# Four graph layers in one plan, mask terms of 256 columns, and biases off TensorE

## The chip, the cores and the metric

The kernel runs on one core of a Trainium2 chip. The core has a matrix engine (TensorE, PE in the profile), a vector engine (VectorE, DVE), a scalar engine for activations (ScalarE, ACT), a general engine (GpSimd, POOL) and a queue that issues DMA transfers (SyncE, SP). The metric is device time of one launch in microseconds; the median over repeated runs is given. Times of single instructions come from one profiled execution.

## The reference

The input is 32 graphs of 512 nodes with 128 features each, one adjacency matrix of 512 x 512 that all graphs share, and the weights of four layers. All numbers are float32. Each layer takes `h = relu(layernorm(x))` and adds its result to `x`:

```
# layer 0: attention over paired scores; softmax over the column's entries
h  = x @ others_weight;  e = leaky_0.1(u1[:, idx1] + u2[:, idx2])
out = softmax(where(adj > 0, e, NEG), axis=1) @ h + x @ self_weight
# layer 1: attention, then a graph network with a two-layer MLP
h = x @ Wp + bp
attn = softmax(where(A <= 0, min, leaky_0.2(s_src[:, None] + s_dst[None, :])))
h_gat = relu(layernorm((attn * A) @ h, g, b))
z = relu(layernorm(((1 + eps) * h_gat + A @ h_gat) @ W1 + b1, g, b))
out = relu(z @ W2 + b2 + h_gat)
# layer 2: attention, elu
out = elu(softmax(where(adj > 0, leaky_0.2(f1[:, None] + f2[None, :]), NEG)) @ (x @ W) + bias)
# layer 3: two projections mixed by one 512 x 512 softmax A that all graphs share
out = diag(A) * (x @ W0) + offdiag(A) @ (x @ W1) + bias
```

In layer 0 the paired indices make the scores of the second 256 nodes (rows) independent of the row: for these rows the attention weight of a column is one number per column where the adjacency has an edge, and nothing elsewhere.

## The kernel before

All 32 graphs stay in SBUF in `xs`, as four blocks of 128 nodes by 128 features per graph. A constant part prepares transposed adjacency (`adjT`), masks, weights with two score columns appended (`w0_ext`, `w1_ext`, `w2_ext`, 130 columns), and layer 3's shared attention matrix (`offT`, `adiag`).

Work is not written in loops that run in order. Each layer of each graph is a *chain* of operations: `op(engine, length, emit, reads, writes)` puts one on a list with an assumed length, and `Plan.run` then goes through all of them, takes at each step the operation that could begin first by its own running estimate (among those within 0.05 us the one with the earliest *turn*, a due time), and emits its instructions. That order is fixed with dependencies, so each engine executes its instructions in the order in which the plan emitted them. Two things limit the choice: a window of chains (`WINDOW = 7`; no chain more than seven past the oldest unfinished one may start), and rooms of buffers. A room is a pool with a count: `banks` are the eight PSUM banks, `scored` 5, `scores` 8, `turned` 4, `by_pool` 5, `by_act` 6 and `by_dve` 5 tiles in SBUF. The two preparing chains, `prepare` and `prepare_last`, run *beside* the others with due times of their own (`PREPARED`, `FILLED`) and leave two PSUM banks free.

The chains are listed as 32 graphs of layer 0 (due every 6.6 us), then 32 of layer 1 (every 13.3), then layers 2 and 3 together, layer 3 four graphs behind layer 2 (7.0 and 6.0).

Every layer begins with `preln`: mean and variance on DVE (`variances`), a power of -0.5 on GpSimd (`inv_dev`), normalisation on GpSimd (`xn`), four transposes on PE, and a relu on ACT into `hT`. Then:

- `layer0` projects `hT` with 130 columns (`project_scored`, four blocks), sends the score columns to another arrangement by four small DMAs (`u`), computes exponentials (`y`) for the first 256 nodes' weights, and scales the projected rows into two copies: `hs` by the sums for the first half and `hs2` for the second. `emit_po` (lines 776 and 784) then sums in one PSUM bank: per block of rows one matmul of `hT` with the self weight, and four with `y` (first two blocks) or with `mask2T`, a 0/1 mask (last two). DVE adds all of it to `xs` at line 790.
- `layer1` uses `project_scored` and `attend` (scores, exponentials, transposes, product with `adjT`, `po` at line 640), a layer norm from PSUM, the product with `adjTe` (`pg`, line 834), and two projections `pz` and `px` (line 535). Its biases `bp` and `b1` enter on PE: each is split into three bf16 terms in rows 0 to 2 of a tile (`b3_p`, `b3_1`), and a matmul of these with a tile that has ones in three rows (`ones3`) opens the sum: line 552 with 260 columns, twice, and line 530 with 512.
- `layer2` is `attend` without weights, and the elu. `layer3` multiplies the transposed input with the diagonal (`own`), projects (`p1`), and sums `own` and `offT` products (lines 897 and 901); DVE adds the residual (`yo`), and SP stores it.

Of the kernel before, what the change touches and what calls it, by code (L numbers as in the profile page):

```python
# [27 lines left out]
BF16 = mybir.dt.bfloat16  # L29
AF = mybir.ActivationFunctionType  # L30
# [3 lines left out]
P = 128  # L34
# [4 lines left out]
WINDOW = 7  # L39
# [14 lines left out]
PREPARED, FILLED = (40.0, 1.0), (400.0, 4.0)  # L54

RAMP, LAG = 4.0, 4
# [41 lines left out]
class Plan:  # L98
# [44 lines left out]
    def run(self):  # L143
# [15 lines left out]
        for _ in range(len(self.ops)):  # L159
# [3 lines left out]
            for engine, ops in ready.items():  # L163
                could = []
                for op in ops:
# [11 lines left out]
                    for room, n in rooms.items():  # L177
                        if len(room.free) < n + (room.reserve if beside else 0):
                            begin = None
                            break  # L180
# [49 lines left out]
def kernel(  # L230
# [110 lines left out]
    mask2T = const("mask2T", (P, C, N2))  # L341
# [12 lines left out]

    b3_p = const("b3_p", (P, P2), BF16)
    b3_1 = const("b3_1", (P, P), BF16)
    ones3 = const("ones3", (P, P), BF16)
# [8 lines left out]
    v_bias, v_w1, v_w2, v_wz, v_b3, v_adjTe, v_rows, v_mlp = (Value() for _ in range(8))  # L366
# [158 lines left out]
    def project(hT, w, reads, b3=None, name="p"):  # L525
        pt = value(banks, name)

        def emit():
            if b3 is not None:
                nc.tensor.matmul(  # L530
                    pt.t, lhsT=ones3, rhs=b3.rearrange("p (o f) -> p o f", o=1).to_broadcast([P, C, P]),
                    start=True, stop=False,
                )
            for c in range(C):
                nc.tensor.matmul(  # L535
                    pt.t[:, c, :], lhsT=column(hT, c), rhs=w,
                    start=(b3 is None), stop=(b3 is None or c == C - 1),
                )

        op(PE, 0.9 + (0.22 if b3 is not None else 0.0), emit, [hT, *reads], [pt])  # L540
        return pt

    def project_scored(hT, w_ext, reads, b3=None):

        h = parts(scored, "h", 2)
        for k in range(2):
            pt = value(banks, "proj")

            def emit(k=k, pt=pt):
                p = pt.t.rearrange("p (c t) f -> p c (t f)", c=2)[:, :, 0:P2]  # L550
                if b3 is not None:
                    nc.tensor.matmul(
                        p, lhsT=ones3, rhs=b3.rearrange("p (o f) -> p o f", o=1).to_broadcast([P, 2, P2]),
                        start=True, stop=False,
                    )
                for c in range(2):
                    nc.tensor.matmul(  # L557
                        p[:, c, :], lhsT=column(hT, 2 * k + c), rhs=w_ext,
                        start=(b3 is None), stop=(b3 is None or c == 1),
                    )  # L560

            op(PE, 0.46 + (0.11 if b3 is not None else 0.0), emit, [hT, *reads], [pt])
# [686 lines left out]
```

## Time and profile before

| | us |
|---|---|
| median of 3 runs | 1117.56 (1116.08 to 1118.26) |
| the profiled execution | 1114.53 |
| its span from first to last instruction | 1112.8 |
| PE busy in layer 0's stretch, 112 to 224 us | 112.00 of 112 |
| PE busy in layer 1's stretch, 280 to 600 us | 316.3 of 320 |
| PE busy in layers 2 and 3, 760 to 1000 us | 239.99 of 240 |

The profile is one execution. A row of the cost table gives a line of the kernel, the engine, the output and inputs by name, their shapes, the count, the busy time (overlaps counted once) and the mean length of one instruction. Matmuls are pipelined and overlap, so a row's mean is longer than the distance between two of them. PEld is the loading of the stationary operand, which runs beside PE. Each f32 matmul appears as two pairs of PEld and PE; a transpose appears as one. In the table of slices each digit is a tenth of a fortieth of the span. The last words of a row say what the engine waited for before it.

### The profile page before, as it was taken

The page shows a single profiled execution, that of the slowest core. Times are in us where ns is not written, and L with a number is a line of the kernel's source. Part 1 is how long each engine was busy: PE and PEld are TensorE (multiplying, and loading weights), DVE is VectorE, ACT ScalarE, POOL GpSimd, SP SyncE. Part 2 cuts the span into 40 slices and gives each one's busy share as a digit, 9 for nine tenths or more (in the row PEclk, how much of TensorE's full clock was granted, in tenths as well). Part 3 has the DMA queues.
Part 4 walks back from the last instruction along what each step waited for, and adds up shares of the span by engine and source line. Part 5 has one row for each costly group of instructions (what it writes and reads, how often), then busy time and mean ns, then how long its engine had stood idle before and what let it go on. Part 6 is the DMA issues. An engine that isn't in the chain of part 4 may idle for free.

```text
span 1112.8 us, 25144 instructions
## 1 busy us (share of the span) xinstructions
PE 1085.5 (98%) x8680; PEld 989.0 (89%) x8683; DVE 922.5 (83%) x3822; ACT 672.1 (60%) x1588; POOL 673.2 (60%) x1040
## 2 busy tenths in 40 slices
PE   5999999999999999999999999899999999999998
PEld 4899999998787877887788887899999999999997
DVE  8989899978889898998989897977777777777772
ACT  3456455567365565574656765866667766766661
POOL 8355454554546555646456555687776777777773
PEclk8899999999999999999999999999999999999999
DMA  7202210000000000000000000000100000000001
GB/s 189 58 11 50 43 36 2 2 2 2 1 1 1 1 1 1 1 1 1 1 1 2 1 1 1 1 20 20 30 21 20 21 20 20 20 21 29 21 21 39
DMA packets 56911, 20.50 MB, mean 18 GB/s; under 512 B 21584, under 2 KB 56272, under 8 KB 56784
## 3 DMA queue, kind: packets, MB, share of 16 engines
q1 hardware_dynamic: 56784, 18.90, 6.9%
q8 instruction: 69, 1.13, 0.4%
q14 instruction: 58, 0.48, 0.1%
HBM read 10.43 MB, written 8.39 MB: 17 GB/s over the span
## 4 chain that ended last, share of the span: by engine, by line
PE 75%; DVE 16%; ACT 3%; POOL 2%; issue 1%; SPq 1%; DMA 1%; POOLq 0%; ACTq 0%; DVEq 0%
PE po L640 16%; PE pt L386 13%; PE po L784 10%; PE po L901 10%; PE proj L557 6%; PE pg L834 5%; DVE y L587 4%; PE prow L386 3%; PE po L776 2%; ACT y L620 2%; DVE st L475 2%; PE po L897 2%; PE p L535 2%; DVE pT L629 2%; PE pz L535 1%
## 5 line engine op out<-in xcount | busy, mean ns | idle before, releaser
L640 PE MATMUL po<-h,pT 128*128 128x128 f32 x2048 | 244.2, 275 | 1.7 <-DVE pT L379 1.0
L510 POOL TENSOR_SCALAR xn<-xs,nmean,rstd 128x128 f32<-128x128 f32 x512 | 232.0, 469 | 19.7 <-DVE st L475 9.6
L640 PEld LDWEIGHTS po<-h,pT 128*128 128x128 f32 x2048 | 236.3, 192 | 5.8 <-issue 1.9
L620 ACT ACTIVATE y<-y,nmax 128x512 f32<-128x512 f32 x256 | 181.7, 712 | 41.1 <-DVE nmean L501 20.1
L612 ACT ACTIVATE y<-y,h 128x512 f32<-128x512 f32 x256 | 165.4, 712 | 37.4 <-DVE rmax L587 37.1
L489 POOL TENSOR_TENSOR rstd<-ve,mhalf 128x4 f32<-128x4 f32 x160 | 163.9, 1024 | 13.4
L587 DVE CUSTOM_DVE_ANT_0 y<-prow,bias 128x512 f32<-128x512 f32 x256 | 161.9, 683 | 9.5 <-PE prow L386 9.0
L519 ACT ACTIVATE hT<-pt 128x512 f32<-128x512 f32 x128 | 75.5, 591 | 125.0 <-PE pt L386 123.2
L386 PE MATMUL pt<-ident,y 128*128 128x128 f32 x1024 | 135.1, 274 | 2.5 <-ACT y L620 1.8
L901 PE MATMUL po<-h,offT 128*128 128x128 f32 x1024 | 135.4, 275 | 0.5 <-ACT h L377 0.5
L487 POOL TENSOR_SCALAR ve<-mv 128x4 f32<-128x4 f32 x160 | 36.7, 229 | 160.9 <-DVE rsum L756 57.7
L386 PEld LDWEIGHTS pt<-ident,y 128*128 128x128 f32 x1024 | 115.7, 141 | 20.0 <-ACT y L620 11.4
L834 PE MATMUL pg<-adjTe,hg 128*128 128x512 f32 x256 | 128.2, 593 | 0.0
L901 PEld LDWEIGHTS po<-h,offT 128*128 128x128 f32 x1024 | 124.6, 192 | 0.6 <-ACT h L377 0.6
L475 DVE BATCH_NORM_STATS2 st<-xs 128x6 f32<-128x128 f32 x512 | 109.9, 276 | 1.5 <-POOL xs L879 1.4
L557 PE MATMUL proj<-w_ext,hT 128*128 128x130 f32 x768 | 107.8, 279 | 2.3 <-ACT hT L519 2.3
L557 PEld LDWEIGHTS proj<-w_ext,hT 128*128 128x128 f32 x768 | 97.7, 194 | 6.7 <-ACT hT L519 2.9
L377 ACT COPY h<-proj 128x260 f32<-128x260 f32 x192 | 67.6, 371 | 46.3 <-PE proj L557 40.5
L879 POOL TENSOR_TENSOR xs<-xs,em 128x512 f32<-128x512 f32 x32 | 40.9, 1278 | 81.2 <-DVE em L878 81.2
L386 PE MATMUL pt<-ident,xn 128*128 128x128 f32 x512 | 85.2, 279 | 2.7 <-POOL xn L510 1.9
L629 DVE TENSOR_TENSOR pT<-pt,adjT 128x512 f32<-128x512 f32 x128 | 82.1, 680 | 3.4 <-PE pt L386 3.2
L742 ACT ACTIVATE y<-y,nmax 128x256 f32<-128x256 f32 x128 | 63.8, 501 | 31.1 <-DVE rs L760 14.0
(189 smaller groups left out, 2101.2 us busy)
## 6 DMA issues: line engine op xcount, KB each, us to landing
xs<-in_x_dram SPq DMA_DIRECT2D x32, 256.0 KB, 3.6
out_dram<-yo SPq DMA_DIRECT2D x32, 256.0 KB, 2.2
u<-h SPq DMA_DIRECT2D x128, 0.5 KB, 1.8
bias<-in_adj_dram SPq DMA_DIRECT2D x4, 256.0 KB, 3.3
wts<-in_L_gnn_W_dram SPq DMA_DIRECT2D x3, 64.0 KB, 3.8
rows<-in_L_gnn_bias_dram SPq DMA_DIRECT2D x2, 64.0 KB, 3.3
wt_o<-L_gnn_others_weight_dram SPq DMA_DIRECT2D x1, 64.0 KB, 2.3
wts<-n_L_gnn_self_weight_dram SPq DMA_DIRECT2D x1, 64.0 KB, 3.8
```

The source lines that it names most:

```text
L386: nc.tensor.transpose(dst(k), src(k), ident)
L475: nc.vector.bn_stats(st[:, c, :], src(c))
L489: nc.gpsimd.tensor_tensor(rstd.own, ve, mhalf, ALU.pow)
L510: nc.gpsimd.tensor_scalar(xn.t[:, c, :], src[:, c, :], nmean.own[:, c : c + 1], rstd.own[:, c : c + 1], ALU.add, ALU.mult,)
L557: nc.tensor.matmul(p[:, c, :], lhsT=column(hT, 2 * k + c), rhs=w_ext, start=(b3 is None), stop=(b3 is None or c == 1),)
L587: nc.vector.tensor_tensor_reduce(wide(y[ib].t), wide(prow.t), bias[:, ib, :], 1.0, LOWEST, ALU.add, ALU.max, rmax.own[:, ib : ib + 1],)
L612: nc.scalar.activation(yw, yw, AF.Prelu, alpha=0.2, bias=h[0].t[:, ib, P : P + 1])
L620: nc.scalar.activation(yw, yw, AF.Exp, bias=nmax.own[:, ib : ib + 1], accum_out=ssum[0].own[:, ib : ib + 1])
L640: nc.tensor.matmul(po[ib].t[:, ib, :], lhsT=pT.t[:, jb, :], rhs=h[0].t[:, jb, 0:P], start=(jb == 0), stop=(jb == C - 1),)
L784: nc.tensor.matmul(po[ib].t[:, ib, :], lhsT=w, rhs=(hs if ib < H else hs2).t[:, jb, :], start=False, stop=(jb == C - 1),)
L834: nc.tensor.matmul(wide(pg.t), lhsT=hg.t[:, nb, :], rhs=adjTe[:, nb, :], start=(nb == 0), stop=(nb == C - 1))
L901: nc.tensor.matmul(po[ib].t[:, ib, :], lhsT=offT[:, jb, blk(ib)], rhs=h1.t[:, jb, :], start=False, stop=(jb == C - 1),)
```

## The change

Four things change.

1. **Order.** The chains of all four layers are listed together: for each step, layer 0 of graph n, layer 1 of graph n-5, layer 2 of n-10 and layer 3 of n-13. The window is 20 chains, and chains three or more past the oldest unfinished one must leave one tile in each room (`KEPT`). `prepare_last` is due from 150 us on and no longer from 400.
2. **Layer 0's second half.** `hs2` is cut by a bit mask (`cut`, 12 low bits cleared, on DVE) and the rest taken by a subtraction on GpSimd; ACT copies the cut part. Both lie side by side in tiles `hl` of type float32r, and `mask2T` is float32r too: one matmul with 256 moving columns gives the sums of both parts. The first and the second two blocks of rows now have a PSUM bank each (`po_1`, `po_2`). ACT copies the sums of the small parts out (`rest`), DVE adds the two banks' main parts to `xs` in two additions, and GpSimd adds `rest`.
3. **Layer 1's first bias.** The matmuls of line 552 go. GpSimd adds the centred `row_p` to the projected features in place, and DVE adds the constant `score_p` to the source scores (`src`); `attend` is told where its scores come from.
4. **Layer 1's second bias.** The matmul of line 530 goes. DVE adds `row_1` to `pz` on its way out of PSUM (`zn`); the variance is taken from `zn`, and ACT scales it by `rz` in four activations where DVE multiplied. The splitting into bf16 terms in `prepare` goes.

```diff
-WINDOW = 7
+WINDOW = 20
+OLD, KEPT = 3, 1
...
-PREPARED, FILLED = (40.0, 1.0), (400.0, 4.0)
+PREPARED, FILLED = (40.0, 1.0), (150.0, 1.5)
+GAPS, LAGS = (5.7, 12.9, 7.2, 5.8), (0, 5, 10, 13)
...
-                        if len(room.free) < n + (room.reserve if beside else 0):
+                        if len(room.free) < n + (room.reserve if beside else KEPT if order[k] >= oldest + OLD else 0):
...
-    mask2T = const("mask2T", (P, C, N2))
+    mask2T = const("mask2T", (P, C, N2), F32R)
...
-                if b3 is not None:
-                    nc.tensor.matmul(
-                        p, lhsT=ones3, rhs=b3.rearrange("p (o f) -> p o f", o=1).to_broadcast([P, 2, P2]),
-                        start=True, stop=False,
-                    )
...
+        cut = value(by_dve, "cut")
+        op(DVE, 0.35, lambda: nc.vector.tensor_scalar(
+            cut.t.bitcast(I32), hs2.t.bitcast(I32), -4096, None, ALU.bitwise_and), [hs2], [cut])
+        hi, lo = [], []
+        for hf in range(H):
+            pair = parts(turned, "hl", 2)
+            hi.append(pair[0])
+            lo.append(pair[1])
...
+        def hl(hf):
+            return wide(hi[hf].t).bitcast(F32R).rearrange("p (c t f) -> p c t f", c=H, t=2)
...
+        for hf in range(H):
+            own = slice(hf * H, hf * H + H)
+            op(ACT, 0.31, lambda hf=hf, own=own: nc.scalar.copy(hl(hf)[:, :, 0, :], cut.t[:, own, :]), [cut], [hi[hf]])
+            op(POOL, 0.7, lambda hf=hf, own=own: nc.gpsimd.tensor_sub(
+                hl(hf)[:, :, 1, :], hs2.t[:, own, :], cut.t[:, own, :]), [hs2, cut], [lo[hf]])
...
+        first, second = parts(banks, "po_1", H), parts(banks, "po_2", H)
+        po = [*first, *second]
+        def terms():
+            return second[0].t.rearrange("p (c t) f -> p c t f", c=H)
...
-                        w = mask2T[:, jb, blk(ib - H)]
-                    nc.tensor.matmul(
-                        po[ib].t[:, ib, :], lhsT=w, rhs=(hs if ib < H else hs2).t[:, jb, :],
-                        start=False, stop=(jb == C - 1),
-                    )
+                        nc.tensor.matmul(
+                            terms()[:, ib - H], lhsT=mask2T[:, jb, blk(ib - H)], rhs=hl(jb // H)[:, jb % H],
+                            start=(jb == 0), stop=False,
+                        )
+                if ib >= H:
+                    nc.tensor.matmul(own, lhsT=column(hT, ib), rhs=wts[:, W_S, :], start=False, stop=True)
...
-        op(DVE, 0.6, lambda: nc.vector.tensor_add(xs[:, b], xs[:, b], po[0].t), po, [v_x[b]])
+        rest = value(by_act, "rest")
+        op(ACT, 0.27, lambda: nc.scalar.copy(rest.t[:, 0:H, :], terms()[:, :, 1, :]), second, [rest])
+        dve(0.33, lambda: nc.vector.tensor_add(xs[:, b, 0:H, :], xs[:, b, 0:H, :], first[0].t[:, 0:H, :]),
+            first, [v_x[b]])
+        dve(0.33, lambda: nc.vector.tensor_add(xs[:, b, H:, :], xs[:, b, H:, :], terms()[:, :, 0, :]),
+            second, [v_x[b]])
+        op(POOL, 0.7, lambda: nc.gpsimd.tensor_add(xs[:, b, H:, :], xs[:, b, H:, :], rest.t[:, 0:H, :]),
+           [rest], [v_x[b]])
...
+            nc.vector.tensor_add(src.own, h[0].t[:, :, P], score_p.to_broadcast([P, C]))
+        dve(0.08, emit_src, [*h, v_score_p], [src])
+        op(POOL, 1.25, lambda: nc.gpsimd.tensor_add(
+            h[0].t[:, :, 0:P], h[0].t[:, :, 0:P], row_p.to_broadcast([P, C, P])), [*h, v_row_p], [v_h])
...
-        pz = project(ginT, wz, [v_wz, v_b3], b3_1, "pz")
-        rz = inv_dev(variances(lambda c: pz.t[:, c, :], [pz]))
+        pz = project(ginT, wz, [v_wz], "pz")
         zn = value(by_dve, "zn")
-        op(DVE, 0.6, lambda: nc.vector.tensor_mul(zn.t, pz.t, per_chunk(rz.own)), [pz, rz], [zn])
+        op(DVE, 0.6, lambda: nc.vector.tensor_add(zn.t, pz.t, row_1.to_broadcast([P, C, P])), [pz, v_row_1], [zn])
+        rz = inv_dev(variances(lambda c: zn.t[:, c, :], [zn]))
+        def emit_zn():
+            for c in range(C):
+                nc.scalar.activation(zn.t[:, c, :], zn.t[:, c, :], AF.Copy, scale=rz.own[:, c : c + 1])
+        op(ACT, 1.16, emit_zn, [rz], [zn])
...
-    order = [(layer0, 6.6, b) for b in range(B)] + [(layer1, 13.3, b) for b in range(B)]
-    for b in range(B + LAG):
-        if b < B:
-            order.append((layer2, 7.0, b))
-        if b >= LAG:
-            order.append((layer3, 6.0, b - LAG))
+    order = []
+    for n in range(B + LAGS[-1]):
+        for layer, gap, lag in zip((layer0, layer1, layer2, layer3), GAPS, LAGS):
+            if 0 <= n - lag < B:
+                order.append((layer, gap, n - lag))
```

## The prediction

> **What bounds the kernel now.** I read the page from the top: busy shares, slices, chain.
>
> ```profile
> span 1112.8 us, 25144 instructions
> PE 1085.5 (98%) x8680; PEld 989.0 (89%) x8683; DVE 922.5 (83%) x3822; ACT 672.1 (60%) x1588; POOL 673.2 (60%) x1040
> ...
> PE   5999999999999999999999999899999999999998
> ...
> DVE  8989899978889898998989897977777777777772
> ...
> PEclk8899999999999999999999999999999999999999
> ...
> PE 75%; DVE 16%; ACT 3%; POOL 2%; issue 1%; SPq 1%; DMA 1%; POOLq 0%; ACTq 0%; DVEq 0%
> ```
>
> TensorE is busy in all slices but the first, at a full clock after the second, and three quarters of the chain are its own. A busy PE need not be one at its peak, so I checked its rate by stage.
>
> ```profile
> core 0: us, PE busy (x) PEld busy (x) DVE busy (x) ACT busy (x) POOL busy (x), PEclk, DMA share, GB/s
> 0.00:28.00 28.00, 15.44 (x93) 13.23 (x94) 23.11 (x132) 10.22 (x24) 22.84 (x47) 0.85 0.74 188
> 28.00:56.00 28.00, 26.37 (x201) 25.11 (x202) 26.53 (x147) 13.43 (x48) 10.43 (x19) 0.90 0.27 57
> ...
> ```
>
> ```profile
> 112.00:224.00 112.00, 112.00 (x1008) 111.95 (x1007) 101.81 (x541) 60.30 (x211) 54.58 (x108) 1.00 0.12 21
> 280.00:400.00 120.00, 118.38 (x824) 96.40 (x825) 106.02 (x410) 66.29 (x141) 62.51 (x86) 1.00 0.00 1
> 400.00:600.00 200.00, 197.94 (x1345) 157.93 (x1344) 180.57 (x711) 117.58 (x253) 114.21 (x159) 1.00 0.00 1
> 760.00:1000.00 240.00, 239.99 (x2128) 235.78 (x2128) 179.34 (x661) 164.41 (x352) 177.73 (x276) 1.00 0.07 21
> ```
>
> Layer 0 (112 to 224 us): 1008 instructions in 112 us, 0.111 us each, without a gap. Layers 2 and 3 (760 to 1000): the same, 0.113. Layer 1 (280 to 600): PE waits 3.7 us of 320, with DVE at 90%. So each PE instruction taken out of the stream is worth its slot. DVE is next, at 91% in layer 0, 90% in layer 1 and only 75% in layers 2 and 3: layer 3 gives it little to do.
>
> What one instruction costs is read from starts in the timeline, since durations overlap:
>
> ```profile
> 344.43 1.88 PE L834 MATMUL pg<-adjTe,hg 128*128 128x512 f32 x4
> 346.15 0.27 PE L552 MATMUL proj<-b_p,ones 128*128 128x260 bf16 x1
> 346.26 0.61 PE L557 MATMUL proj<-w_ext,hT 128*128 128x130 f32 x4
> 346.71 0.27 PE L552 MATMUL proj<-b_p,ones 128*128 128x260 bf16 x1
> 346.82 0.61 PE L557 MATMUL proj<-w_ext,hT 128*128 128x130 f32 x4
> ...
> 349.45 0.38 PE L530 MATMUL pz<-b,ones 128*128 128x512 bf16 x1
> 349.67 1.05 PE L535 MATMUL pz<-wz,ginT 128*128 128x128 f32 x8
> ```
>
> A bf16 matmul of 260 columns holds PE for 0.11 us, one of 512 for 0.22, an f32 one of 512 columns for 0.43 (1.72/4), and each f32 matmul of the source is two instructions.
>
> ```profile
> L784 PE MATMUL po<-hs,mask2T 128*128 128x128 f32 x512 | 67.6, 275 | 0.0
> ...
> L552 PE MATMUL proj<-b_p,ones 128*128 128x260 bf16 x64 | 17.5, 274 | 0.0
> ...
> L530 PE MATMUL pz<-b,ones 128*128 128x512 bf16 x32 | 12.1, 379 | 0.0
> ```
>
> The 512 instructions on mask2T are 256 matmuls (2 row blocks, 4 column blocks, 32 graphs).
>
> **What the Trainium skill says.** FP8 and Floating Point Precision, "TensorE Precision Notes": true FP32 takes four passes through the array; a reduced FP32 reads the 4 bytes and truncates. The trace agrees with the first: 2 x 0.111 us per 128 columns is four times 128 columns at 2.4 GHz (0.053). No run here shows the reduced form. TensorE: Matmul & The Clock Gate, "Back-to-back issue gap": N/2.4 + 2.5 ns when warm, so 0.109 us for 256 columns in one pass; the bf16 rows (0.11 for 260, 0.22 for 512) agree. GPSIMD Engine Reference, "Key points": GpSimd contends for SBUF with VectorE instructions of two SBUF inputs or in a 2-port mode. No cost of this shows: the fused add and maximum on DVE took 683 ns in layer 1 with GpSimd 56% busy and 684 in layers 2 and 3 with it 74% busy.
>
> **The change, part by part** (per graph, then 32 graphs).
>
> Mask terms of layer 0. Gone: 8 matmuls of 128 columns, 16 x 0.111 = 1.78 us. Added: 8 single-instruction matmuls of 256 columns, the high and low part of a value side by side. Below: 0.109 us each (one pass). Above: 0.22, the bf16 row of 512 columns, if the reduced form takes two cycles a column. I take 0.12: one pass, plus a little because loads of 32-bit weights last 141 to 192 ns against 98 for bf16. New 0.96, gain 0.82, over 32 graphs 26.1 us (28.9 to 0.5).
>
> Biases of layer 1. Gone: two bf16 matmuls of 260 columns and one of 512, 2 x 0.11 + 0.22 = 0.44 us, over 32 graphs 14.1. All of it is PE time. PE work falls by 40.2 us.
>
> What the other engines get:
> - DVE: the mask of the bits (`cut`, 128x512 in SBUF) 0.45 by the rows of `bias` (443 ns) and `num` (479); two adds of 256 columns for one of 512, at most +0.1; `src` 0.16. `zn` is an add where it was a multiply. +0.7, over 32 graphs 22; minus some 5 of the one-time bf16 splitting. 922 becomes about 940.
> - ACT: two copies of 256 elements and `rest` at 0.35 each (`h<-proj`, 67.6/192), 1.05; four scaled copies of 128. ScalarE: Activation LUTs, "What ACT_TABLE_LOAD costs", prices an ACTIVATE with one pointer operand at 279 + 0.833N ns, 93 of it overlapped: 0.29 each, 1.17. +2.2, over 32 graphs 71: 743.
> - GpSimd: two subtractions and one add of 256, half of the 1.28 us row and a little, 0.7 each, and an add of 512, 1.28. +3.4, over 32 graphs 108: 781.
>
> In a span near 1075 these are 87%, 69% and 73% of busy time; PE stays first. The added steps also lengthen chains: about 2 us between `hs2` and the second half of layer 0, 1 us at its end (GpSimd's add follows an ACT copy), 1.5 us around `zn`. What covers them is work of other graphs, if PE has it in its order. The issue order of the changed kernel interleaves all four layers and is free of long one-graph stretches, so I cost them at nothing; with the cover gone they would be 4.5 us a graph.
>
> The plan. Once layer 3 runs, one graph of each layer goes by together: PE 31.3 us (6.23 from the L0 timeline rows - 0.82; 13.33 in layer 1 - 0.44; 13.10 for layers 2 and 3, the period of `po L640` in the chain), DVE about 28.0 (5.65, 12.0 and 9.8 from the windows, +0.6): 89%, where layers 0 and 1 stood before at 90 to 91% with PE waiting 0 to 1.2%. Of the 7.8 us that PE idled from 224 to 760 I take 6 back.
>
> Against that stands the head. Layer 0 after the change has 5.4 us of PE and 6.1 of DVE, layer 1 12.9 and 12.2, layer 2 7.2 and 7.3: until layer 3 joins, DVE is the bound. I counted the instructions of the issue order ahead of the first `own` product of layer 3 by their rows: 228 us on PE, 253 on DVE (its rows overlap; the sum is scaled by 0.871, which brings the same count of the kernel before to its 922.5). At 97% use, DVE needs 261: PE loses 33 us there. Before, the first 56 us lost 14 to idling and 5 to the lower clock, and the other DVE-heavy stretch, layer 0, lost nothing. Some 6 of the 33 come back because the order lets PE work ahead on other chains. Net +8.
>
> SP: output stores now stand between x loads and the small `u` transfers of layer 0, so a store that waits for `yo` holds both back. Loads run some 8 graphs ahead and a `u` takes 1.8 us of a lag of a dozen graphs: nothing. Constants for layer 3 are prepared earlier; that is in the head's count.
>
> Sum: -40.2 - 6 + 8 = -38 us. The profiled execution took 1114.5 us (1112.8 span and 1.7 around it): 1076.5. The median is 3.0 above it, so 1079.
>
> **Rivals.**
> 1. The reduced matmul takes 0.22 us, or its weight load isn't hidden: the mask part gains nothing, 1079 + 26 = 1105. For it: nothing in the trace shows the form. Against: f32 transposes, 4 bytes wide, run at one instruction per 0.111.
> 2. DVE's bound lasts longer: it reaches 91%, as in layer 0, not 97%, in the head (253/0.91 = 278, +17) and costs 0.3 us of waits per steady slot (+7): 1103. For it: every layer but one leans on DVE. Against: DVE ran at 95% from 28 to 56 us.
> 3. Slower: the wider window starves PE of PSUM banks. Layer 0 now holds two of the eight for its sums, layers 1 and 2 hold one each from first block to normalisation, through a GpSimd power of 1.02 us; with 20 chains admitted instead of 7, older work waits for banks that younger chains hold. Price: 38 us are eaten at 1.2 us of waits per slot of 31.3; with 2 us, 1079 + 64 = 1143. Against: layer 1, alone with seven chains, lost 1.2% of PE, and one slot of each room is kept for the oldest chains.
>
> That the change doesn't do what it says is excluded: its instructions stand in the order.
>
> **How the numbers follow.** Forecast 0.70 (1079, own range 1062 to 1095), rival 1 0.10, rival 2 0.10, rival 3 0.10. Between: gains below the forecast's come from 0.109 us and no head loss, 1079 - 3 - 8 - 2 = 1066, less a few for the clock. Eight in ten: 1060 to 1105. The first three cases end faster; a sliver of rivals 2 and 3 lands within 0.2% (2.2 us, about what a measurement here can tell): faster 0.88, same 0.02, slower 0.10.
>
> **What would show it.** Matmuls on `hl` as 256 instructions of 128x256 starting about 0.11 us apart, not 512 nor 0.22; no matmul on `ones`; PE busy about 1045 us; DVE near 940; PE idle only in the first quarter, with DVE at 9 in those slices and PE not; one period of about 31.3 us from the twelfth graph on. It is wrong if PE idles in the middle of the span with PSUM readers as releasers, or if the period is above 33 us.

## The result, and the profile after

| | before | after |
|---|---|---|
| median of 4 runs, us | 1116.89 (1116.08 to 1118.26) | 1108.93 (1107.21 to 1110.34) |
| ratio, 95% interval | | 0.9927 (0.9909 to 0.9945) |
| profiled execution / its span, us | 1114.53 / 1112.8 | 1108.71 / 1107.0 |

The kernel became 8 us faster, not 38. The first part of the page of the changed kernel, its slices of PE, DVE and the clock:

```profile
span 1107.0 us, 24781 instructions
PE 1062.2 (96%) x8332; PEld 958.5 (87%) x8333; DVE 976.8 (88%) x3900; ACT 733.9 (66%) x1812; POOL 794.3 (72%) x1168
...
PE   6889898999999999999999999999999999999996
...
DVE  7999999999998999899999999999989887877762
...
PEclk7899999999999999999999999999999999999998
```

VectorE was to be busy for about 940 us and has 976.8; TensorE was to have 1045 and has 1062. PE's digits fall to 8 in the first quarter, where DVE stands at 9, and to 6 in the last slice. A digit of 9 hides whether a tenth is missing, so the stretches are needed (the columns: stretch, its length, then busy time and instructions of PE, PEld, DVE, ACT and POOL, clock, DMA). Windows of the changed kernel:

```profile
core 0: us, PE busy (x) PEld busy (x) DVE busy (x) ACT busy (x) POOL busy (x), PEclk, DMA share, GB/s
50.00:300.00 250.00, 233.26 (x1731) 200.15 (x1730) 247.85 (x1000) 167.37 (x448) 176.33 (x252) 1.00 0.04 8
300.00:1000.00 700.00, 695.33 (x5620) 636.99 (x5619) 626.17 (x2479) 496.67 (x1203) 522.63 (x761) 1.00 0.05 13
...
1080.00:1107.00 27.00, 17.29 (x109) 15.16 (x108) 5.55 (x16) 3.08 (x5) 10.20 (x16) 0.80 0.07 20
```

The same stretch of the kernel before:

```profile
50.00:300.00 250.00, 249.20 (x2138) 239.78 (x2139) 223.22 (x1113) 141.82 (x443) 123.12 (x212) 1.00 0.10 21
```

From 50 to 300 us VectorE went from 89% to 99% and TensorE from 249.2 us to 233.3. In the last 27 us PE is idle for 9.7 and its clock is 0.80.

Busy time still counts a slowed matmul as work. So I give each matmul the distance between two starts of its kind in the timeline (0.112 us for an f32 instruction of 128 columns, 0.109 for a transpose, 0.43 for 512 columns, 0.12 for the new form) and call the sum PE's *content*; what is left of a stretch is *lost*. All in us:

| lost in | 0 to 50 | 50 to 300 | 300 to 1000 | from 1000 | sum | content |
|---|---|---|---|---|---|---|
| before | 24.1 | 1.1 | 20.0 | 7.9 | 53.2 | 1059.6 |
| after | 25.1 | 26.7 | 16.4 | 19.1 | 87.3 | 1019.7 |

Content fell by 39.9, and lost time rose by 34.1. The span fell by the difference, 5.8. The removed PE work was real, and most of it came back as lost time, in the head and in the tail.

What made VectorE so busy is in its cost groups (busy us, mean ns | idle before). Of the changed kernel:

```profile
L594 DVE SCALAR_TENSOR_TENSOR nmax<-top 128x4 f32<-128x4 f32 x64 | 34.8, 544 | 0.2
...
L694 DVE TENSOR_TENSOR lt<-u 128x2 f32<-128x2 f32 x32 | 23.8, 743 | 0.0
...
L766 DVE TENSOR_SCALAR cut<-hs 128x512 int32<-128x512 int32 x32 | 13.2, 414 | 0.0
```

and of the kernel before:

```profile
L501 DVE TENSOR_SCALAR nmean<-mv 128x4 f32<-128x4 f32 x128 | 31.1, 246 | 0.3
...
L602 DVE SCALAR_TENSOR_TENSOR nmax<-top 128x4 f32<-128x4 f32 x64 | 19.2, 301 | 0.4
...
L702 DVE TENSOR_TENSOR lt<-u 128x2 f32<-128x2 f32 x32 | 5.0, 157 | 0.9 <-DMA u<-h 0.4 <-issue 0.4
```

`cut` is new work, and costs what was forecast. `lt`, two numbers per partition, is the same instruction on the same data in both kernels and went from 157 ns to 743. The timeline tells why. VectorE in the changed kernel (start, length):

```profile
567.20 1.22 DVE L594 SCALAR_TENSOR_TENSOR nmax<-top 128x4 f32<-128x4 f32 x1
...
577.16 1.31 DVE L694 TENSOR_TENSOR lt<-u 128x2 f32<-128x2 f32 x1
```

and GpSimd at the same moments:

```profile
566.68 1.73 POOL L922 TENSOR_TENSOR xs<-xs,em 128x512 f32<-128x512 f32 x1 [1.73 <-DVE top L590]
...
577.19 1.26 POOL L864 TENSOR_TENSOR hn<-hn,rows 128x512 f32<-128x512 f32 x1
```

Each time both end together: 568.42 and 568.41, 578.47 and 578.45. The small VectorE instruction, whose operands both lie in SBUF, lasts until GpSimd's addition of two SBUF tensors is over. I sum over all VectorE instructions what each lasts beyond the usual short length of its own kind (the 15th percentile and 0.03 us), and call it *excess*: 31.6 us before, 83.8 after, of which in the stretch from 50 to 300 us 4.7 before and 29.4 after. In the changed kernel 124 VectorE instructions have more than 0.1 us of it. Of these, 81 end within 0.04 us of the end of a GpSimd operation on two tensors of 256 or 512 columns, and they hold 65 of the 82 us.

Two operands are not the only case. `nmean` (line 501 before) scales four numbers per partition and has a single operand in SBUF. In the kernel before, 28 of its 128 executions began while a GpSimd addition had about 0.5 us or more to run; all 28 lasted 0.51 to 0.89 us, to the end of that addition, where the median is 0.165. They are a third of the excess before.

### The profile page after: what moved, and what is told of

Its sections match the earlier page's. It is cut to its first block, busy times and chain, and to the rows that moved or that the text cites. A ratio compares the mean times of both kernels' runs of the same rounds, so it can differ in the third digit from the quotient of the medians.

```text
span 1107.0 us, 24781 instructions
## 1 busy us (share of the span) xinstructions
PE 1062.2 (96%) x8332; PEld 958.5 (87%) x8333; DVE 976.8 (88%) x3900; ACT 733.9 (66%) x1812; POOL 794.3 (72%) x1168
## 5 line engine op out<-in xcount | busy, mean ns | idle before, releaser
L632 PE MATMUL po<-h,pT 128*128 128x128 f32 x2048 | 241.4, 275 | 2.4 <-DVE pT L621 1.3
L518 POOL TENSOR_SCALAR xn<-xs,nmean,rstd 128x128 f32<-128x128 f32 x512 | 237.9, 479 | 6.8 <-DVE st L483 2.1
L871 PE MATMUL pg<-adjTe,hg 128*128 128x512 f32 x256 | 131.0, 593 | 0.0
L604 ACT ACTIVATE y<-y,src 128x512 f32<-128x512 f32 x128 | 84.3, 713 | 54.4 <-DVE rmax L579 54.3
L604 ACT ACTIVATE y<-y,h 128x512 f32<-128x512 f32 x128 | 85.7, 715 | 18.1 <-DVE rmax L579 17.0
L922 POOL TENSOR_TENSOR xs<-xs,em 128x512 f32<-128x512 f32 x32 | 48.8, 1525 | 67.4 <-DVE top L590 32.4
L394 PE MATMUL pt<-ident,xn 128*128 128x128 f32 x512 | 83.6, 283 | 6.3 <-POOL xn L518 5.5
L916 POOL TENSOR_TENSOR v<-v,rows 128x512 f32<-128x512 f32 x32 | 40.9, 1278 | 65.7 <-DVE v L915 54.1
```

Source lines behind the costliest of these rows:

```text
L394: nc.tensor.transpose(dst(k), src(k), ident)
L518: nc.gpsimd.tensor_scalar(xn.t[:, c, :], src[:, c, :], nmean.own[:, c : c + 1], rstd.own[:, c : c + 1], ALU.add, ALU.mult,)
L604: nc.scalar.activation(yw, yw, AF.Prelu, alpha=0.2, bias=src()[:, ib : ib + 1])
L632: nc.tensor.matmul(po[ib].t[:, ib, :], lhsT=pT.t[:, jb, :], rhs=h[0].t[:, jb, 0:P], start=(jb == 0), stop=(jb == C - 1),)
L871: nc.tensor.matmul(wide(pg.t), lhsT=hg.t[:, nb, :], rhs=adjTe[:, nb, :], start=(nb == 0), stop=(nb == C - 1))
```

## Experiments

Each kernel below is the changed one with the edit shown, unless it says otherwise. Times are medians of 4 or 5 runs; ratios are against the kernel before on the same chip. Lost and excess come from one profiled execution each. Every edit makes the planner order everything anew, so a few us in one stretch are no evidence by themselves.

| label | us | ratio, 95% | content | lost 0-50, 50-300, 300-1000, 1000- | excess |
|---|---|---|---|---|---|
| before | 1116.89 | 1 | 1059.6 | 24.1, 1.1, 20.0, 7.9 | 31.6 |
| after | 1108.93 | 0.9927 (0.9909-0.9945) | 1019.7 | 25.1, 26.7, 16.4, 19.1 | 83.8 |
| e1 operations alone | 1134.37 | 1.0156 (1.0140-1.0172) | 1019.9 | 25.0, 43.3, 35.8, 8.1 | 63.7 |
| e2 order alone | 1120.80 | 1.0031 (1.0011-1.0052) | 1060.2 | 26.8, 4.5, 10.3, 16.6 | 81.6 |
| e6 masks alone | 1124.71 | 1.0061 (1.0039-1.0082) | 1033.8 | 28.4, 14.5, 27.1, 15.9 | 88.7 |
| e7 biases alone | 1098.06 | 0.9829 (0.9813-0.9846) | 1046.4 | 19.4, 5.1, 7.9, 18.4 | 45.3 |
| e3 more two-input adds | 1137.54 | 1.0182 (1.0165-1.0199) | 1019.9 | 27.5, 30.7, 38.5, 19.9 | 112.5 |
| e4 more one-input ops | 1122.64 | 1.0043 (1.0026-1.0061) | 1019.9 | 23.9, 29.4, 29.0, 20.1 | 99.2 |
| e5 scaling by ScalarE | 1111.12 | 0.9948 (0.9933-0.9964) | 1019.9 | 21.4, 21.5, 26.7, 19.1 | 99.1 |
| e8 shorter lags | 1142.13 | 1.0228 (1.0207-1.0248) | 1019.9 | 25.6, 29.1, 36.8, 28.7 | 81.3 |
| m0 no side work | 1083.83 | 0.9709 (0.9693-0.9725) | 1019.9 | 24.9, 13.4, 6.2, 17.9 | 48.3 |
| m1 GpSimd's half | 1089.10 | 0.9754 (0.9735-0.9773) | 1019.9 | 21.5, 21.8, 5.3, 18.6 | 67.4 |
| m2 the cut's half | 1090.64 | 0.9773 (0.9754-0.9791) | 1019.9 | 22.2, 17.6, 10.5, 17.2 | 64.5 |
| c1 loads, no series | 1097.78 | 0.9827 (0.9807-0.9847) | 1019.9 | 23.6, 20.3, 12.6, 18.3 | 72.7 |
| c2 no cut | 1093.82 | 0.9800 (0.9785-0.9815) | 1019.9 | 23.1, 20.7, 12.9, 17.6 | 73.7 |
| c3 no cut, lag 14 | 1086.70 | 0.9728 (0.9712-0.9744) | 1019.9 | 23.9, 16.0, 11.1, 16.0 | 67.7 |
| c4 one operand | 1091.81 | 0.9781 (0.9766-0.9796) | 1019.9 | 27.2, 19.7, 6.9, 18.4 | 61.9 |
| c5 both, lag 14 | 1086.59 | 0.9720 (0.9697-0.9742) | 1019.9 | 24.5, 25.8, 3.0, 13.1 | 64.6 |
| c6 both, lag 15 | 1092.18 | 0.9768 (0.9740-0.9796) | 1019.9 | 24.5, 25.8, 7.5, 13.5 | 67.6 |
| e9 biases alone, lag 14 | 1097.59 | 0.9831 (0.9812-0.9849) | 1046.4 | 19.4, 9.9, 6.1, 13.8 | 45.0 |

### Which part of the change does what

e1 keeps the plan of the kernel before (layer after layer, window 7) with the new operations; e2 is the other half, e6 and e7 the new order with one of the two parts.

```diff
-WINDOW = 20
-OLD, KEPT = 3, 1
+WINDOW = 7
+OLD, KEPT = 3, 0
...
```

> The new operations in the old order (window of 7 chains, layer 0 for all graphs, then layer 1, then 2 and 3 together, layer 3 four graphs behind). Theory A (VectorE is the bound wherever layer 3 is missing, and waits for GpSimd's two-input adds make it longer): the 40 us taken from TensorE come back only in part, since layer 0 now needs 6.1 us of VectorE and some waits for 5.4 of TensorE, and layer 1 about as much of either; 32 x 6.7 + 32 x 13.3 + 32 x 13.1 and some 45 for preparation, head and tail give about 1105, VectorE busy near 970. Theory B (the new order is what costs): about 1117 - 40 = 1078, with TensorE without gaps in layer 0's stretch.

e2 has the operations of the kernel before and the plan of the changed one:

```diff
-WINDOW = 7
+WINDOW = 20
+OLD, KEPT = 3, 1
...
+GAPS, LAGS = (5.7, 12.9, 7.2, 5.8), (0, 5, 10, 13)
...
```

> The old operations in the new order. TensorE's content is that of the kernel before, 1060 us. Theory A: VectorE has less to do and fewer waits than with the new operations (busy near 935), so the head costs TensorE some 30 us and not 51, but the ill-filled tail of 15 to 18 us stays: 1060 + 30 + 18 + 18, about 1126, slower than before. Theory B (the new order itself makes the head, whatever the operations): the head costs 51 us again, about 1147. If the new order is good by itself: 1110 or less.

e6 leaves the biases on PE:

```diff
-        h = project_scored(hT, w1_ext, [v_w1])
+        h = project_scored(hT, w1_ext, [v_w1, v_b3], b3_p)
...
-        pz = project(ginT, wz, [v_wz], "pz")
+        pz = project(ginT, wz, [v_wz, v_b3], b3_1, "pz")
...
```

> The new order and the mask terms of 256 columns; layer 1's biases stay matmuls on TensorE. TensorE's content 1034 us. Theory A: layer 0's added VectorE work makes part of the head's loss, layer 1 is not lengthened: lost from 50 to 300 us about 15 (27 with both, 5 with neither), the time about 1112.

e7 leaves the mask terms as f32 matmuls of 128 columns:

```diff
-                            terms()[:, ib - H], lhsT=mask2T[:, jb, blk(ib - H)], rhs=hl(jb // H)[:, jb % H],
-                            start=(jb == 0), stop=False,
...
+                        w = mask2T[:, jb, blk(ib - H)]
...
```

> The new order and layer 1's biases on GpSimd and VectorE; the mask terms stay f32 matmuls of 128 columns. TensorE's content 1046 us. Theory A: some 8 us lost from 50 to 300 us, the time about 1117: 4 us of the 14 taken from TensorE are left over the order alone (1121).

The order alone gains nothing: its middle loses 10 us less, its tail 9 more. Without it the new operations cost 1.6%: with layer 0 by itself, 43 us are lost between 50 and 300. With the order, the biases bring 22.7 us (1120.8 to 1098.1), of which 13.8 are content. The masks bring 26.7 us of content and *cost* 10.9 (1098.1 to 1108.9). Without the biases (e6) they cost 3.9 (1120.8 to 1124.7), with 26.4 of content gone. Of the four expectations the first sum for e2, 1126, came near; those for e1, e6 and e7 missed by 13 to 29 us. They took the loss of the new operations in the old order and of the masks too low, and the gain of the biases too low. Windows and groups of e7:

```profile
50.00:300.00 250.00, 249.03 (x1916) 221.61 (x1915) 236.21 (x1003) 168.38 (x431) 157.82 (x223) 0.99 0.04 7
```

```profile
L594 DVE SCALAR_TENSOR_TENSOR nmax<-top 128x4 f32<-128x4 f32 x64 | 20.3, 317 | 0.3
...
L694 DVE TENSOR_TENSOR lt<-u 128x2 f32<-128x2 f32 x32 | 6.2, 194 | 2.8 <-DMA u<-h 2.8
```

With VectorE at 94% instead of 99%, PE has its 249 us in the head. And `lt` takes 194 ns in e7, though all of GpSimd's additions of 512 columns are there: where in a plan's period the small instruction falls decides it. In e2, with the operations of before, it takes 693 ns. Of its 32 executions 19 are held to the end of such an addition in the changed kernel, 16 in e2, one in e7, and none before; the others all stay under 0.34 us.

### Is it the side work of the masks, and which of it

m0 leaves out what is cut away from `hs2`: the matmul reads `hs2`, written in the reduced form, twice, and `cut`, `hl`, `rest` and the last addition are gone.

```diff
-                            terms()[:, ib - H], lhsT=mask2T[:, jb, blk(ib - H)], rhs=hl(jb // H)[:, jb % H],
+                            terms()[:, ib - H], lhsT=mask2T[:, jb, blk(ib - H)], rhs=hs2.t[:, jb : jb + 1, :].bitcast(F32R).to_broadcast([P, 2, P]),
...
```

> Of the mask part only what TensorE does is left: its matmuls of 256 columns read hs2 itself, rounded to float32r and twice side by side; the cutting of hs2, the copies and subtractions that fill hl, and the copy and GpSimd addition of rest are left out (so the small parts of layer 0's second half are missing). TensorE's content stays at 1020 us. Theory C (the 26 us of TensorE are real, and the side work on VectorE, ScalarE and GpSimd undoes them): near 1098 - 26 = 1072 (up to 1080 with the smaller head). Rival (TensorE's new matmuls or the second PSUM bank cost elsewhere): stays above 1095.

m1 has GpSimd's subtractions (of `hs`, with no cut; the matmuls read the difference twice), `rest` and the addition; m2 has the cut and ScalarE's copies, and nothing of GpSimd's.

```diff
-                hl(hf)[:, :, 1, :], hs2.t[:, own, :], cut.t[:, own, :]), [hs2, cut], [lo[hf]])
+                hl(hf)[:, :, 1, :], hs2.t[:, own, :], hs.t[:, own, :]), [hs2, hs], [lo[hf]])
...
```

> As before it, but GpSimd's side work is back: two subtractions of 256 columns into hl (hs2 less hs), the copy of rest and its addition on GpSimd; the cut and the copies of the main part stay out (the matmuls read the subtracted part twice; values of layer 0 differ). Theory C1 (GpSimd's two-input operations hold VectorE up): 15 to 25 us above the run without both, VectorE busy up by 15 or more though it has nothing more to do. Theory C2 (VectorE's own added work is what counts): within 8 us of the run without both.

```diff
-            op(POOL, 0.7, lambda hf=hf, own=own: nc.gpsimd.tensor_sub(
-                hl(hf)[:, :, 1, :], hs2.t[:, own, :], cut.t[:, own, :]), [hs2, cut], [lo[hf]])
...
```

> The cut on VectorE (0.41 us a graph) and ScalarE's two copies into hl are back; GpSimd's subtractions and the rest's copy and addition stay out (the matmuls read the main part twice; values of layer 0 lack the small parts). Theory C1: within 10 us of the run without both. Theory C2: 15 us or more above it.

The head in m0's windows:

```profile
50.00:300.00 250.00, 241.97 (x1831) 212.72 (x1830) 242.67 (x1028) 168.41 (x438) 158.86 (x226) 0.99 0.04 9
```

The matmuls alone save 14.2 us against e7, half of their content; 1072 to 1080 was expected. VectorE stands at 97% in the head already, and PE loses 13.4 us there (5.1 in e7). m0 keeps the second PSUM bank and the new matmuls, so these don't undo the gain. Each half of the side work costs 5 to 7 us, both cost 25.1. Neither theory ahead of m1 and m2 fits: each gave 15 us or more to one half and 10 at most to the other. The excess adds up almost exactly (48.3, +19.1 and +16.2 make 83.6; with both it is 83.8); the time does not. So c1 kept all the side work but broke the series (GpSimd's difference is computed and not read, the matmuls read the main part twice), and c2 kept the series but for its first step: ScalarE writes `hs2` in the reduced form into `hl`, and GpSimd subtracts what was written, so that the sum of both parts is kept.

```diff
-                hl(hf)[:, :, 1, :], hs2.t[:, own, :], cut.t[:, own, :]), [hs2, cut], [lo[hf]])
+                hl(hf)[:, :, 1, :], hs2.t[:, own, :], hs.t[:, own, :]), [hs2, hs], [lo[hf]])
...
-                            terms()[:, ib - H], lhsT=mask2T[:, jb, blk(ib - H)], rhs=hl(jb // H)[:, jb % H],
+                            terms()[:, ib - H], lhsT=mask2T[:, jb, blk(ib - H)], rhs=hl(jb // H)[:, jb % H, 0:1, :].to_broadcast([P, 2, P]),
...
```

> All the side work of the mask part at once (cut, two copies, two GpSimd subtractions, rest), but not in series: the subtractions read hs2 and hs and nobody waits for them, the matmuls read the main part twice (values of layer 0 lack the small parts). The loads are those of the changed kernel, the chain is that of the run with the cut alone (1091). Theory L (the loads together fill VectorE and hold it up): 1103 to 1110, VectorE busy near 975. Theory K (the series of VectorE, GpSimd and TensorE in each graph of layer 0 delays it): 1098 or less.

```diff
...
-            op(ACT, 0.31, lambda hf=hf, own=own: nc.scalar.copy(hl(hf)[:, :, 0, :], cut.t[:, own, :]), [cut], [hi[hf]])
+            op(ACT, 0.31, lambda hf=hf, own=own: nc.scalar.copy(hl(hf)[:, :, 0, :], hs2.t[:, own, :]), [hs2], [hi[hf]])
...
-                hl(hf)[:, :, 1, :], hs2.t[:, own, :], cut.t[:, own, :]), [hs2, cut], [lo[hf]])
+                hl(hf)[:, :, 1, :], hs2.t[:, own, :], hl(hf)[:, :, 0, :]), [hs2, hi[hf]], [lo[hf]])
```

> The cut on VectorE is left out: ScalarE writes hs2 as float32r, and GpSimd subtracts what was written. 13 us less of VectorE, the same number of GpSimd and ScalarE instructions, the series is as long as before. Theory L: VectorE below the point where it fills up, as in the runs with one half of the side work: 1092 to 1098. Theory K: 1105 to 1109.

Load without the series costs 14 us over m0, and the series without the cut's load 10; neither is the 25 of both. Taking away 13 us of VectorE work (c2) brings 15 us; VectorE's busy time falls by 22, as 10 us of excess go with it. c1 came where the series was to be the cause, c2 where the load was to be it. How much of the 25 us is load and how much is the longer series stays open.

### Are the waits for GpSimd a cause

e3 does the addition `hgb` three times: 64 more GpSimd adds of two SBUF inputs, and not one more VectorE instruction. e4 is meant as its control: three one-input operations in place.

```diff
+        op(POOL, 1.25, lambda: nc.gpsimd.tensor_add(hgb.t, hg.t, row_of(B_2)), [hg, v_rows], [hgb])
+        op(POOL, 1.25, lambda: nc.gpsimd.tensor_add(hgb.t, hg.t, row_of(B_2)), [hg, v_rows], [hgb])
```

> The changed kernel with GpSimd's addition of hgb in layer 1 done three times (the same result written again), 64 more two-input adds, 82 us more of GpSimd. Theory A (small VectorE instructions that read two operands from SBUF wait until a two-input GpSimd add has ended): VectorE busy rises by 15 to 35 us from 977 with not one VectorE instruction more, and the time by 5 to 15 us. Rival (GpSimd's lateness is what counts, not the sharing): VectorE busy stays at 977 within 4.

```diff
+        for _ in range(3):
+            op(POOL, 0.85, lambda: nc.gpsimd.tensor_scalar(hgb.t, hgb.t, 0.0, 1.0, ALU.add, ALU.mult), [], [hgb])
```

> The changed kernel with three in-place one-input operations of 512 elements on hgb per graph of layer 1 (adding 0, times 1), 96 more, some 70 to 110 us more of GpSimd. Theory A: one-input operations do not hold VectorE back: VectorE busy stays near 977 (within 8) and the time within 5 us of 1109. Rival (GpSimd's load itself is what counts): time and VectorE rise as with the two-input adds.

Busy times of e3, from its page:

```profile
PE 1068.8 (94%) x8333; PEld 958.9 (84%) x8333; DVE 1005.1 (88%) x3900; ACT 732.1 (64%) x1812; POOL 885.3 (78%) x1232
```

VectorE's busy time rose from 976.8 to 1005.1 us with the same 3900 instructions, and the time by 28.6. The time was expected to rise by 5 to 15. But the control is not clean: in e4, where 8 and 5 at most were expected, VectorE rose by 15.5 us and the time by 13.7. Against the GpSimd work added (91 us in e3, 69 in e4), that is 0.31 and 0.23. So two inputs on GpSimd do more, and one input is not free: in e4, 24 VectorE instructions with 9 us of excess end together with one of the added operations. The series and the new plan are in both numbers.

c4 goes the other way and takes the two worst-placed small instructions away from the collision: `lt` becomes a reduction with one operand, and ScalarE makes `nmax` of `attend`.

```diff
-            nc.vector.scalar_tensor_tensor(nmax.own, ntop.own, 0.2, ntop.own, ALU.mult, ALU.min)
+            nc.scalar.activation(nmax.own, ntop.own, AF.Prelu, alpha=0.2, scale=-1.0)
+            nc.scalar.activation(nmax.own, nmax.own, AF.Copy, scale=-1.0)
...
-            nc.vector.tensor_add(lt1.own, u.own[:, :, 0], u.own[:, :, 1])
+            nc.vector.tensor_reduce(lt1.own, u.own, AX.X, ALU.add)
```

> The changed kernel, but two of the small VectorE instructions that GpSimd's adds hold up no longer read two operands from SBUF: lt1 is a reduction over its one input, and nmax goes to ScalarE (two small activations). Together they waited some 42 us in the changed kernel. Theory L: VectorE busy falls by 25 us or more, and the time by 5 to 12, to about 1100. Rival (the waits move on to the next instruction of two operands, since the plan's pattern repeats): VectorE busy falls by less than 15, the time stays within 4 us.

Busy times of c4, from its page:

```profile
PE 1052.8 (96%) x8333; PEld 958.0 (88%) x8333; DVE 949.2 (87%) x3836; ACT 754.4 (69%) x1940; POOL 790.1 (72%) x1168
```

It gained 17.1 us, more than the 5 to 12 expected. VectorE's busy time fell by 27.6 us, though the 64 instructions moved away have only some 0.12 us each of their own (7.7 us); excess makes up 21.9. The reduction in c4's groups:

```profile
L695 DVE TENSOR_REDUCE lt<-u 128x2 f32<-128x4 f32 x32 | 4.7, 146 | 0.3 <-DMA u<-h 0.3
```

743 ns became 146. That is no luck of phase: in c4, c5 and c6 together 32 of these reductions began while a GpSimd addition had 0.3 to 1.3 us to run, and none lasted over 0.16 us. Part of the wait moved on: the next step on `lt`, which still has two operands, now holds 16.9 us of excess.

e5 tested the rival that VectorE's work as a whole is too much: ScalarE does the two products `hs` and `hs2`, and VectorE loses 64 instructions of 0.68 us, 43 us.

```diff
-        op(DVE, 0.6, lambda: nc.vector.tensor_mul(hs.t, h[0].t[:, :, 0:P], per_chunk(rs.own)), [rs, *h], [hs])
-        op(DVE, 0.6, lambda: nc.vector.tensor_mul(hs2.t, h[0].t[:, :, 0:P], per_chunk(rs2.own)), [rs2, *h], [hs2])
+        def emit_scaled(dst, by):
+            for c in range(C):
+                nc.scalar.activation(dst.t[:, c, :], h[0].t[:, c, 0:P], AF.Copy, scale=by.own[:, c : c + 1])
+        op(ACT, 1.16, lambda: emit_scaled(hs, rs), [rs, *h], [hs])
+        op(ACT, 1.16, lambda: emit_scaled(hs2, rs2), [rs2, *h], [hs2])
```

> The changed kernel with hs and hs2 of layer 0 scaled by ScalarE (four activations each with the sum as scale) where VectorE multiplied; 1.36 us less on VectorE and some 2.3 us more on ScalarE per graph. Theory A (in the head, until layer 3 joins, VectorE is the bound): the 15 graphs of layer 0 in the head free some 20 us of VectorE; TensorE loses under 10 us from 56 to 287 us where it lost 26, VectorE busy falls to about 935, and the time to about 1090. Rival (the head is bound by the order and by latencies, not by VectorE): VectorE busy falls all the same, the time stays within 4 us of 1109.

A miss: 1111 us. The head in e5's windows:

```profile
50.00:300.00 250.00, 238.32 (x1770) 206.75 (x1771) 234.58 (x979) 203.90 (x562) 175.38 (x256) 0.99 0.04 9
```

Only 18.5 us of VectorE's time went (976.8 to 958.3), in part because the excess rose by 15; VectorE was at 94% in the head, and PE still lost 21.5 us there and 10 more in the middle. In the head, then, VectorE's total isn't the only thing that holds PE up once the series is longer on another engine.

What goes with PE's loss there is the excess. Over the 20 executions of the table the two, both taken from 50 to 300 us, have a correlation of 0.94 (e2 and e7: about 11 us of excess, 5 lost; the changed kernel: 29 and 27). With VectorE's busy time the correlation is 0.60, with GpSimd's 0.85. Which of these drives the others it doesn't show; c4, which takes excess away with the least other change, gains 7 of its 17 us in this stretch.

### The lags

```diff
-GAPS, LAGS = (5.7, 12.9, 7.2, 5.8), (0, 5, 10, 13)
+GAPS, LAGS = (5.7, 12.9, 7.2, 5.8), (0, 3, 6, 10)
```

> The changed kernel with lags of 3, 6 and 10 graphs in the place of 5, 10 and 13: layer 3 joins three graphs earlier, and stands four graphs behind layer 2 at the end. Theory A: the head that VectorE bounds is shorter (20 us lost from 50 us until layer 3 runs, not 27), and at the end one more graph of layer 3 fills the last chains of layer 2 (10 us lost after 1000 us of the span's order, not 18): about 1095. Rival (chains that follow each other so closely wait for their forerunner): the steady period rises above 32 us, and the time is 1109 or more.

Shorter lags bring layer 3 in earlier and were meant to shorten the head; all stretches lost more, the tail too (28.7), and VectorE waited 15.6 us for the DMA of `u` ahead of `lt`. About 1095 was expected. e9 is e7 with layer 3 one graph later, c3 is c2 with the same, c5 is c2 and c4 and the same, and c6 has one graph more.

```diff
-GAPS, LAGS = (5.7, 12.9, 7.2, 5.8), (0, 5, 10, 13)
+GAPS, LAGS = (5.7, 12.9, 7.2, 5.8), (0, 5, 10, 14)
```

> The new order and layer 1's biases off TensorE, masks as before (1098 us), with layer 3 four graphs behind layer 2 and not three. The tail of the run with lag 13 lost 18 us after 1000 us; with one more graph of layer 3 left for the last chains of layer 2 it should lose 8 to 12, the time 1090 (up to 1098 if the order found by the plan is worse elsewhere). It would beat both kernels.

> The same with layer 3 four graphs behind layer 2: at most 4 us less than with three, as the biases alone showed nothing (1097.6 to 1098.1); 1090 to 1098 by theory L. It would beat both kernels.

> Both savings of VectorE time together (no cut, and the two held-up instructions replaced), layer 3 four graphs behind layer 2. VectorE busy 925 to 940. Theory L: 4 to 10 us under the version without the replacement, 1077 to 1083. If VectorE is no longer the bound in the head, little more is gained: 1084 to 1088.

> The same with layer 3 five graphs behind layer 2. TensorE loses 16 to 18 us after 1000 us in nearly all runs; one more graph of layer 3 at the end should take 2 to 5 of it, while layer 3 joins one graph later at the head: between 4 us faster and 4 us slower than with 14.

The tail shrinks by 1.6 us from c2 to c3 and by 4.6 from e7 to e9. e9 gives it back in the head, and its time is the same within the interval; c3 gains 7.1, mostly outside the tail, where at most 4 were expected. c5, with 5.5 us less VectorE time than c3, is no faster, as was expected if VectorE no longer bounds the head; but its head loses 25.8 us where c3's loses 16.0. One graph more (c6) costs 5.6 us, with nearly the same tail; 4 either way were expected. c3 and c5, 1086.7 and 1086.6, compute all that the changed kernel does and are 2.0% faster than it (22 of 1108.9 us).

## Why the prediction was right in sign and wrong in size

Against the profiled execution the prediction was 1076.5 us, and 1108.7 came. By the terms of its sum:

| term | predicted | measured |
|---|---|---|
| PE content, masks and biases | -40.2 | -39.9 |
| head, to 300 us | +8 | +26.6 |
| middle, 300 to 1000 us | -6 | -3.6 |
| tail, from 1000 us | none | +11.2 |
| sum | -38 | -5.7 |

**The content was right.** The timeline of PE in the changed kernel:

```profile
515.94 0.72 PE L802 MATMUL po<-hl,mask2T 128*128 128x256 f32 x4
516.50 0.38 PE L807 MATMUL po<-wts,hT 128*128 128x128 f32 x2
```

The four instructions on `hl` and the turn to the next kind take 0.56 us, where 0.22 us for each would be 0.88. Within the 64 groups of four the median distance of two starts is 0.120 us, the value taken. That refutes rival 1.

**The head failed**, at the step "I counted the instructions of the issue order ahead of the first `own` product of layer 3 by their rows: 228 us on PE, 253 on DVE", with "No cost of this shows" ahead of it. PE's count was right: its content up to its first matmul on `own` is 227.5 us. But it got there at 278.6 us, not at 261. VectorE had reached the product `own` at 268.9, 8 us late, after 259 us of work, and PE then still had 9.7 us of other work ahead of its matmul on `own`. The step took PE's loss as 261 less 228, as if both engines came to `own` together; the loss was 278.6 less 227.5, 51 us. In the kernel before PE's matmul also came 7.7 us after that product, and in e7, e9, m0, c3 and c5 9 to 12. The 253 took each VectorE instruction at a length of the kernel before, in which it seldom met a two-input addition of GpSimd (4.7 us of excess in 50 to 300, now 29.4). Some 29 of the 259 us up to `own` are excess. The rows of before carry 31.6 us of it in 922.5, about 9 in 253 by my estimate. So the rest of the count was some 14 us too high, and that the sum came within 6 us was luck. And the 6 us that PE was to win back by working ahead are not there: by 300 us it had lost 51.8 us, where 27 were allowed (33 - 6). The added steps, "I cost them at nothing", were not covered either: with the cut and GpSimd's half each alone they cost 5 to 7 us, with both 25 (m0, m1, m2).

Why did the trace of before show me no cost of sharing? I tested with the fused add and maximum, 683 and 684 ns, which reads one operand from PSUM. In the changed kernel the longest of its 256 executions is 692 ns, though 22 of them began with 0.8 us or more of a GpSimd addition still to run: it takes no part in the collisions. The Trainium skill, GPSIMD Engine Reference, "Key points", names VectorE instructions with two SBUF inputs or in a 2-port mode, and says nothing of the amount. The trace agrees on two inputs (`lt`, 743 ns), and shows no instruction's mode. I chose an instruction with one input in SBUF. Line 602's row stood in the answer for before, 301 ns for four numbers per partition, with a longest of 1262 against a median of 150: the cost was visible, in the spread and not in the mean. So it was in line 501's, 890 against 165.

So rival 2 (VectorE's bound lasts longer, 1103) came nearest in place and in size, but not in its reason: up to 268.9 us VectorE was busy for 96% of the time, not for 91; its instructions were longer. Rival 3 (PSUM banks) has no support: PE lost less in the middle than before, and no starvation shows there. The period was to be 31.3 us (its terms add to 31.4); the stores from 574.7 to 797.0 us are seven periods, 31.77 each.

**The tail was missing.** Layer 3 of a graph runs only three graphs behind layer 2, where it ran four behind, so the last graphs of layer 3 stand alone. PE at the end of the changed kernel (idle before, and its releaser, in brackets):

```profile
1083.16 0.90 PE L394 MATMUL pt<-ident,xn 128*128 128x128 f32 x2 [2.62 <-POOL xn L518]
1084.54 0.90 PE L394 MATMUL pt<-ident,xn 128*128 128x128 f32 x2 [0.48 <-POOL xn L518]
1086.85 2.07 PE L538 MATMUL p<-wts,hT 128*128 128x128 f32 x8 [1.41 <-ACT hT L527]
...
1096.46 1.16 PE L538 MATMUL p<-wts,hT 128*128 128x128 f32 x8 [0.29 <-ACT hT L527]
```

PE waits for GpSimd's normalisation and ScalarE's relu of one graph with nothing else to do, and after these gaps the eight matmuls of `p` take 2.07 us; ten us later they take 1.16. The granted clock was 0.50 from 1082.8 to 1093.0 us. The last stretch of the kernel before, at 0.99 (columns as above):

```profile
1085.00:1112.80 27.80, 22.64 (x199) 22.01 (x197) 6.64 (x17) 3.09 (x5) 8.52 (x13) 0.99 0.13 39
```

That the tail belongs to the order is shown: 8.1 us lost with the old plan (e1), 16.6 with the new one (e2), whatever the operations. The distance of three graphs makes the waits of the last 27 us: PE loses 14 to 15.5 us there in all 13 runs with the new plan and this distance, and 5 to 6.5 where layer 3 runs four or five graphs behind layer 2 (e9, c3, c5, c6), as with the old plan (before 5.9, e1 6.1). In those four runs the clock stays at 0.96 or more. But from 1000 us up to there they lose 7 to 10 us, where the 13 lose 1 to 4.5, so that the whole tail shrinks by 2 to 5 only (c2 to c3, e7 to e9). e8, four graphs behind layer 2 too, loses 8.2 in the last 27 us and 20 ahead of them. Why the stretch ahead is worse with more distance stays open.

## What to carry to other kernels

When work moves from the bounding engine to two others, count the others' time with their collisions, not by the means of a profile in which they seldom met: look at the longest and the median of the smallest instructions, and ask which of them grow while GpSimd adds two tensors (here those with both operands in SBUF, and one scaling with a single operand). Where VectorE stood at 97 to 99% in the head (m0, e6, the changed kernel), work taken out of the first engine brought less than its slot, so price it by stretch, and price the last stretch of a new order too, where the pipeline runs dry. A change that consists of parts is best priced part by part: here the order with the biases alone was worth more than the whole.

## What the runs showed of the hardware

- A VectorE instruction on 128x2 or 128x4 numbers with two operands in SBUF, 0.15 us by itself, lasts up to 1.3 us when it meets a GpSimd addition of two 128x512 tensors: both end within 0.02 us of each other in the two pairs shown. A reduction of the same numbers from one operand takes 146 ns, also beside such an addition (32 cases in c4, c5 and c6, none over 160). One operand isn't always enough: the scaling `nmean` was held to the end of the addition in 28 of 28 cases before, and lasted 0.51 to 0.89 us.
- Which instruction pays is a matter of phase: `lt` took 157 ns before, 743 after, 194 in e7 and 158 in m0, on the same data. Half of its 32 executions in the changed kernel lasted 0.69 us or more.
- A one-input operation of GpSimd holds VectorE up too: 24 instructions in e4, 9 us in all, ended with one of the added operations.
- A float32r matmul of 256 columns starts 0.120 us after the one before it, 0.008 more than an f32 instruction of 128 columns, of which a matmul needs two.
- In the tail a gap of 2.62 us on PE (1080.5 to 1083.2 us) came with a granted clock of 0.50 from 1082.8 to 1093.0 us.
